# Splitting minus the row maxima into three bfloat16 parts: on VectorE behind the last reduction, or as a queued piece on GpSimd

## The chip, the cores and the metric

The kernel runs on one core of a Trainium2 chip. The metric is the device time of one execution in microseconds. Before the change three runs took 3936.0, 3942.05 and 3945.19 us; the median is 3942.05 us. Engine names below are those of the profile: PE is TensorE, DVE is VectorE, ACT is ScalarE, POOL is GpSimd, SP is the engine whose queue issues most of the DMAs.

## The reference, cut to what matters

One transformer layer over 4 sequences of 2048 tokens, width 256: modulation, layer norm, attention with 16 heads of 16, residual, layer norm, a mixture of 16 experts (4 per token) plus a shared expert, residual. The change touches only the softmax of the attention:

```python
q = _apply_rotary(q, rope)
k = _apply_rotary(k, rope)
scores = jnp.einsum('bhqd,bhkd->bhqk', q, k) * scale
scores = jnp.where(causal_mask, -jnp.inf, scores)
attn = jax.nn.softmax(scores, axis=-1)
out = jnp.einsum('bhqk,bhkd->bhqd', attn, v)
```

The softmax subtracts the maximum of each row of scores before the exponential. The kernel computes that maximum first, in a separate pass over the scores, and then adds its negative to the scores inside the matmul that makes them a second time.

## The kernel before, in words

**Blocks and groups.** The 8192 tokens are 16 blocks of 512 (`n`), four to a sequence. The heads are 4 groups of 4 (`g`). A pair (n, g) is one group of attention work, 64 in all. `units` puts them in order: the first sequence has 16 units of one group each, the other three have units of two groups each.

**A step.** The main loop takes a unit in steps of 128 keys. A step has on PE four small matmuls that add minus the maximum to a PSUM buffer `st` (L1055, from `mt`), four matmuls of the scores (L1062), on ACT two exponentials `e` (L1070), on POOL, for the last four steps of a group only, two triangular masks on `e` (L1074), and, one step late, the matmuls `po` with the values (L1003, in `weigh`). There are 640 steps.

**The maxima.** While a unit runs, the row maxima of the next unit are made beside it, by the generator `row_max`: PE writes scores into a PSUM buffer `ps` (L803, L826), and DVE reduces it to a column of `mparts` (L813, L836). `st` and `ps` share three PSUM buffers of two banks each. `draw` pulls these pieces so that they are spread over the steps of the unit, and what is left is drained at its end. After the last reduction of a group, `row_max` reduces the columns to minus the maximum, `negm` (L849, 128 x 16 numbers), and splits that into three bfloat16 parts in `mb`: round (L857), subtract what was rounded (L859), round the rest (L860), and both once more. Five DVE instructions follow the reduction directly.

**From the parts to the step.** `row_max` then adds a generator `max_rows` to the queue `after_max`. Its first piece does nothing; its second transposes `mb` on PE (`pmx`, L869) and copies the result to `mt` on ACT (L871). The planner pulls one piece of `after_max` at the end of a step, if the credit allows. If a group is about to begin and its `mt` has not been made, the remaining pieces are pulled on the spot.

**The planner.** `Background` holds queues of generators. Before every piece a generator yields what the piece needs: PSUM banks of the small pool `wps` (one buffer), microseconds of DVE, microseconds of POOL. `Budget` adds credit at each step, and `fill` pulls a piece only while the credit it needs is positive. The pieces of `row_max` are pulled by `draw` whatever the credit is, but what they name is taken from it. The other queues are `ahead` (the `prologue` of later blocks: norm, projection, rotation, split into high and low halves, with POOL at L678, L725, L734), `over` and `ends` (dividing and output projection), and `after` (`send`: norm, routing and the scatter of rows by indirect DMAs on POOL, L489). The order of the instructions on PE, ACT, DVE and POOL is what this program emits; each engine works through its own list in that order.

After the attention the expert stage follows, from about 2787 us of the profiled execution on; nothing in it is changed.

Of the kernel before, what the change touches and what calls it, by code (L numbers as in the profile page):

```python
# [14 lines left out]
ALU = mybir.AluOpType  # L15
# [105 lines left out]
def adaln_attention_moe(  # L121
# [17 lines left out]
    nc = tc.nc  # L139
# [457 lines left out]
    with ExitStack() as actx:  # L597
# [38 lines left out]
        mparts, mbs = [], []  # L636
# [154 lines left out]
        def row_max(n, g):  # L791

            qb = n % NQ
            qt, kt = qts[n, g], kts[n, g]
            turn_ = len(turns) % 2
            turns.append((n, g))
            parts = mparts[turn_]
            for q in range(2):

                def scores(ps, t, key, width, to, start=True, stop=True):  # L800
                    for half in range(2):
                        rows = slice(64 * half, 64 * half + 64)
                        nc.tensor.matmul(  # L803
                            ps[:, half, to : to + width],
                            lhsT=qt[rows, q, t * P : (t + 1) * P],
                            rhs=kt[rows, q, key : key + width],
                            start=start,
                            stop=stop,
                            skip_group_check=True,
                        )  # L810

                def best(ps, to, width):
                    nc.vector.tensor_reduce(to, ps[:, :, :width], AX.X, ALU.max)  # L813

                mine = parts[:, 2 * q : 2 * q + 2]
                for kb in range(qb):
                    for t in range(4):
                        yield 0, 1.15, 0
                        ps = psp.tile([P, 2, BT], F32, tag="s", name="ps")
                        scores(ps, t, kb * BT, BT, 0)  # L820
                        best(ps, mine[:, :, t, 2 + kb], BT)
                yield 0, 1.15, 0
                ps = psp.tile([P, 2, BT], F32, tag="s", name="ps")

                for half in range(2):
                    nc.tensor.matmul(  # L826
                        ps[:, half, :],
                        lhsT=idb,
                        rhs=mask.rearrange("p t k -> p (t k)"),
                        start=True,  # L830
                        stop=False,
                        skip_group_check=True,
                    )
                for t in range(4):
                    scores(ps, t, qb * BT + t * P, P, t * P, start=False, stop=(t == 3))
                nc.vector.tensor_reduce(  # L836
                    mine[:, :, :, 0],
                    ps.rearrange("p h (t k) -> p h t k", k=P),
                    AX.X,
                    ALU.max,  # L840
                )
                for t in range(1, 4):
                    yield 0, 0.15 + 0.27 * t, 0
                    ps = psp.tile([P, 2, BT], F32, tag="s", name="ps")
                    scores(ps, t, qb * BT, t * P, 0)
                    best(ps, mine[:, :, t, 1], t * P)
            yield 0, 1.1, 0
            negm = tp.tile([P, 2, 2, 4], F32, tag="negm", name="negm")
            nc.vector.tensor_reduce(  # L849
                negm.rearrange("p q h t -> p (q h) t"),  # L850
                parts[:, :, :, : 2 + qb],
                AX.X,
                ALU.max,
                negate=True,
            )
            mb = mbs[turn_].rearrange("p t (h q e) -> p q h t e", h=2, q=2)
            nc.vector.tensor_copy(mb[:, :, :, :, 0], negm)  # L857
            for part in (1, 2):
                nc.vector.tensor_sub(negm, negm, mb[:, :, :, :, part - 1])  # L859
                nc.vector.tensor_copy(mb[:, :, :, :, part], negm)  # L860
            after_max.add(max_rows(n, g, mbs[turn_]))

        def max_rows(n, g, mb):

            yield 0, 0, 0
            yield 1, 0, 0
            pm = wps.tile([P, 2, BT], BF, tag="w", name="pmx")
            for t in range(4):
                nc.tensor.transpose(pm[:, 0, t * P : (t + 1) * P], mb[:, t, :], idb)  # L869
            mt = tp.tile([P, BT], BF, tag="mt", name="mt", bufs=3)  # L870
            nc.scalar.copy(mt, pm[:, 0, :])  # L871
            mts[n, g] = mt
# [84 lines left out]
        ahead, maxes, after_max, over, ends, after = (Background(budget) for _ in range(6))  # L957
# [4 lines left out]
        load(0)  # L962
        load(1)
        maxes.add(row_max(*units[0][0]))
        maxes.drain()
        after_max.drain()
# [52 lines left out]
        for u, unit in enumerate(units):  # L1019
# [8 lines left out]
            if u + 1 < len(units):  # L1028
                left = max_pieces(units[u + 1])
                for n, g in units[u + 1]:  # L1030
                    maxes.add(row_max(n, g))
# [10 lines left out]
            for s_, (n, g, k_, nkt, off) in enumerate(steps_):  # L1042
# [46 lines left out]
                part = (BT - off) / BT  # L1089
# [412 lines left out]
```

## Time and profile before

| what | value |
|---|---|
| median of three runs | 3942.05 us |
| the profiled execution, its own time | 3947.4 us |
| its span, first to last instruction | 3945.6 us |
| busy: PE, PEld, DVE, ACT, POOL | 84%, 44%, 65%, 39%, 39% of the span |
| attention, 138 to 2787 us of the span | 2649 us |
| groups of attention work | 64 |

PEld is the load of weights on TensorE, which runs beside the matmuls. In the groups of instructions, "x128 | 53.0, 414" reads: 128 instructions, 53.0 us of busy time, 414 ns for one on average. In a timeline, a line gives the start, the time taken, the engine, the line of the kernel, and in brackets how long the engine had been idle and what ended that.

### The profile page before, as it was taken

How to read it: one execution, taken by the hardware profiler on the slowest of the kernel's cores; microseconds unless marked ns; L12 is line 12 of the kernel's file. 1: busy time of each engine (PE TensorE's matmuls, PEld its weight loads, DVE VectorE, ACT ScalarE, POOL GpSimd, SP SyncE). 2: the span in 40 equal slices, each digit the busy share in tenths (PEclk: the TensorE clock that was granted, in tenths of full speed). 3: DMA queues.
4: the chain of work that ended last, by engine and by line, in shares of the span. 5: the costliest groups of instructions: out<-in, count | busy, mean ns of one | idle time of the engine just before them, and what ended most of it. 6: DMA issues, size and time to landing. Idle time of an engine off the chain costs nothing. (4 is left out here: it accounts for less than half of the span.)

```text
span 3945.6 us, 56494 instructions
## 1 busy us (share of the span) xinstructions
PE 3315.9 (84%) x20276; PEld 1727.9 (44%) x20400; DVE 2583.1 (65%) x4644; ACT 1525.7 (39%) x2188; POOL 1531.1 (39%) x2222
## 2 busy tenths in 40 slices
PE   3567888888888989988898888899788889899994
PEld 1223333333334433333433333343377677676662
DVE  1344676767776777767767776677276576667775
ACT  0223344544444544544454454455522222222220
POOL 1223243352434342343425334310146556545555
PEclk7668898988999988988999998899999899899997
DMA  4233233341223322233332222220177567678763
GB/s 168 91 101 115 84 128 112 121 147 54 85 96 125 116 94 91 82 108 117 108 110 100 83 99 81 96 73 28 59 272 243 199 231 250 217 270 303 275 252 139
DMA packets 275115, 544.96 MB, mean 138 GB/s; under 512 B 27534, under 2 KB 143246, under 8 KB 274834
## 3 DMA queue, kind: packets, MB, share of 16 engines
q1 hardware_dynamic: 242578, 454.79, 33.9%
q0 software_dynamic: 27648, 77.63, 5.3%
q10 hardware_dynamic: 4608, 8.91, 0.6%
q8 instruction: 161, 2.64, 0.3%
q14 instruction: 120, 0.98, 0.1%
HBM read 351.42 MB, written 189.81 MB: 137 GB/s over the span
## 5 line engine op out<-in xcount | busy, mean ns | idle before, releaser
L1070 ACT ACTIVATE e<-st 128x1024 f32<-128x1024 f32 (+3 forms) x1280 | 1078.8, 895 | 1039.5 <-PE st L1062 960.3
L813 DVE TENSOR_REDUCE mparts<-ps 128x2 f32<-128x1024 f32 (+3 forms) x1152 | 1180.0, 1044 | 457.1 <-PE ps L803 409.4
L803 PE MATMUL ps<-kt,qt 64*128 64x512 f32 (+3 forms) x3328 | 613.6, 414 | 177.9 <-ACT e L1070 66.7
L1003 PE MATMUL po<-e,vg 128*32 128x512 f32 (+3 forms) x5120 | 670.6, 590 | 29.5 <-POOL e L1074 14.8
L803 PEld LDWEIGHTS ps<-kt,qt 64*128 64x128 f32 x3328 | 303.3, 203 | 769.3 <-ACT e L1070 447.3
L1074 POOL TENSOR_SCALAR_AFFINE_SELECT e<-e 128x256 f32<-128x256 f32 x512 | 204.7, 410 | 952.2 <-ACT e L1070 948.1
L1171 PE MATMUL gu<-xT,wt 128*128 128x256 f32 x1920 | 465.4, 397 | 24.1 <-issue 11.4
L1274 POOL DMA_INDIRECT yd<-yt,to x320 | 315.8, 987 | 390.7 <-ACT hb L1182 208.3
L1062 PE MATMUL st<-qt,kt 64*128 64x512 f32 (+3 forms) x2560 | 462.3, 441 | 0.0
L1171 PEld LDWEIGHTS gu<-xT,wt 128*128 128x128 f32 x1920 | 371.3, 198 | 112.9 <-issue 45.5
L1055 PE MATMUL st<-mt,pick 32*128 32x512 bf16 (+3 forms) x2560 | 302.5, 373 | 79.7 <-DVE mparts L813 49.0
L489 POOL DMA_INDIRECT xs<-row,rowx x256 | 248.4, 970 | 177.7 <-DVE row L480 122.7
L836 DVE TENSOR_REDUCE mparts<-ps 128x8 f32<-128x1024 f32 x128 | 156.7, 1224 | 196.8 <-PE ps L803 181.8
L1062 PEld LDWEIGHTS st<-qt,kt 64*128 64x128 f32 x2560 | 206.2, 199 | 138.5 <-issue 126.7
L725 POOL TENSOR_TENSOR r<-qk,rp 128x512 f32<-128x512 f32 x128 | 164.8, 1306 | 189.3 <-DVE qk L702 185.7
L1270 ACT ACTIVATE yt<-y,of 128x256 f32<-128x256 f32 x160 | 67.1, 470 | 403.5 <-DVE is L1250 213.9
L1055 PEld LDWEIGHTS <-pick 32*128 32x128 bf16 x2560 | 87.4, 92 | 303.2 <-issue 291.1
L1003 PEld LDWEIGHTS po<-e,vg 128*32 128x32 f32 x5120 | 109.2, 112 | 186.9 <-issue 129.1
L678 POOL TENSOR_TENSOR low<-whole,high 128x512 fp32r<-128x512 f32 x64 | 81.4, 1271 | 253.7 <-ACT whole L750 253.7
L1209 PE MATMUL y<-wt,ha 128*128 128x256 f32 x640 | 158.6, 389 | 10.8 <-issue 7.7
L698 PE MATMUL pq<-wqkv,hT 128*128 128x512 f32 x256 | 145.1, 694 | 17.4 <-ACT whole L750 14.9
L1209 PEld LDWEIGHTS y<-wt,ha 128*128 128x128 f32 x640 | 118.6, 195 | 32.7 <-issue 14.7
(209 smaller groups left out, 3603.4 us busy)
## 6 DMA issues: line engine op xcount, KB each, us to landing
wt<-in_w_all SPq DMA_DIRECT2D x160, 640.0 KB
kt<-kd SPq DMA_DIRECT2D x124, 512.0 KB
xt<-xs SPq DMA_DIRECT2D x160, 272.0 KB
qt<-qd SPq DMA_DIRECT2D x64, 512.0 KB
yg<-yd SPq DMA_DIRECT2D x16, 2048.0 KB
vg<-vd SPq DMA_DIRECT2D x124, 168.0 KB
xb<-in_x SPq DMA_DIRECT2D x32, 512.0 KB
qd<-high SPq DMA_DIRECT2D x128, 128.0 KB
```

The source lines that it names most:

```text
L489: s_ = nc.gpsimd.indirect_dma_start(out=ph.xs[:, :], out_offset=bass.IndirectOffsetOnAxis(ap=rowx[:, n, t, j : j + 1], axis=0), in_=row[:, ...
L725: nc.gpsimd.tensor_tensor(r_, parts[:, :, :, s].unsqueeze(2).to_broadcast(full), rp[:, qb * 4 + t, s].unsqueeze(1).to_broadcast(full), ALU ...
L803: nc.tensor.matmul(ps[:, half, to : to + width], lhsT=qt[rows, q, t * P : (t + 1) * P], rhs=kt[rows, q, key : key + width], start=start, s ...
L813: nc.vector.tensor_reduce(to, ps[:, :, :width], AX.X, ALU.max)
L1003: nc.tensor.matmul(po[32 * j : 32 * j + 32, off:], lhsT=va[:, k_, j * (HD + 1) : j * (HD + 1) + 32], rhs=es[j // 2][:, j % 2, off:], start ...
L1055: nc.tensor.matmul(sts[q][:, h_, off:], lhsT=pick[rows, :], rhs=mt[rows, off:], start=True, stop=False,)
L1062: nc.tensor.matmul(sts[q][:, h_, off:], lhsT=kt[rows, q, k_ * P : (k_ + 1) * P], rhs=qt[rows, q, off:], start=False, stop=True,)
L1070: nc.scalar.activation(es[q][:, :, off:], sts[q][:, :, off:], AF.Exp, scale=SCALE)
L1074: nc.gpsimd.affine_select(out=es[q][:, :, off : off + P], in_=es[q][:, :, off : off + P], compare_op=ALU.is_ge, fill=0.0, base=0, pattern= ...
L1171: nc.tensor.matmul(ps[:, c_ * TT : (c_ + 1) * TT], lhsT=wt[:, c_, k * 2 * I + cols : k * 2 * I + cols + P], rhs=xT[:, k, c_ * TT : (c_ + 1 ...
L1209: nc.tensor.matmul(pss[half][:, t, :], lhsT=ha[:, at_ : at_ + P], rhs=wt[:, half, 4 * I : 4 * I + D], start=(t == 0), stop=False, skip_gro ...
L1274: s_ = nc.gpsimd.indirect_dma_start(out=ph.yd[:, :], out_offset=bass.IndirectOffsetOnAxis(ap=to[:, t : t + 1], axis=0), in_=yt[:, t, :], i ...
```

## The change

The five DVE instructions after L849 become five POOL instructions with the same operands, and move from `row_max` into `max_rows`, as a first piece that names 1.2 us of POOL credit. The last piece of `row_max` names 0.2 us of DVE credit where it named 1.1.

```diff
-            yield 0, 1.1, 0
+            yield 0, 0.2, 0
             negm = tp.tile([P, 2, 2, 4], F32, tag="negm", name="negm")
             nc.vector.tensor_reduce(
...
             mb = mbs[turn_].rearrange("p t (h q e) -> p q h t e", h=2, q=2)
-            nc.vector.tensor_copy(mb[:, :, :, :, 0], negm)
+            after_max.add(max_rows(n, g, negm, mb, mbs[turn_]))
+
+        def max_rows(n, g, negm, parts, mb):
+
+            yield 0, 0, 1.2
+            nc.gpsimd.tensor_copy(parts[:, :, :, :, 0], negm)
             for part in (1, 2):
-                nc.vector.tensor_sub(negm, negm, mb[:, :, :, :, part - 1])
-                nc.vector.tensor_copy(mb[:, :, :, :, part], negm)
-            after_max.add(max_rows(n, g, mbs[turn_]))
-
-        def max_rows(n, g, mb):
-
+                nc.gpsimd.tensor_tensor(negm, negm, parts[:, :, :, :, part - 1], ALU.subtract)
+                nc.gpsimd.tensor_copy(parts[:, :, :, :, part], negm)
             yield 0, 0, 0
             yield 1, 0, 0
             pm = wps.tile([P, 2, BT], BF, tag="w", name="pmx")
```

`max_rows` has three pieces where it had two: the parts, an empty one, and the transposes with the copy.

## The prediction

> **What bounds the kernel now.** I read the busy time by stage first.
>
> ```profile
> 138.00:865.00 727.00, 591.13 (x3719) 255.85 (x3747) 452.69 (x666) 298.02 (x391) 231.63 (x292) 0.86 0.31 105
> 865.00:2787.00 1922.00, 1697.41 (x11650) 716.08 (x11745) 1369.10 (x2069) 931.25 (x1190) 682.76 (x1012) 0.91 0.27 93
> ```
>
> The columns are the stretch and its length, busy time of PE, PEld, DVE, ACT and POOL, then granted clock, DMA share and GB/s. The rows are the first sequence and the other three. PE is busy 81% and 88%, DVE 62% and 71%, POOL 32% and 36%: PE carries the attention, and only its idle time (136 and 225 us) can be won or added to. Next, the groups of instructions with shapes kept apart, for what is moved:
>
> ```profile
> L859 DVE TENSOR_TENSOR negm<-negm,mb 128x16 f32<-128x16 f32 x128 | 53.0, 414 | 4.4
> L860 DVE CAST mb<-negm 128x16 bf16<-128x16 f32 x128 | 47.7, 373 | 4.4
> ...
> L857 DVE CAST mb<-negm 128x16 bf16<-128x16 f32 x64 | 28.8, 449 | 2.2
> ```
>
> Together 129.5 us for 320 instructions on 16 numbers a partition. The view of one line (least, median, greatest ns) shows that this is not their own price:
>
> ```profile
> L860 DVE CAST mb<-negm x128: 201/204/1262, 138.6 to 2785.9; 128x16 bf16<-128x16 f32 x128
> ```
>
> The timeline shows where the 1.2 us come from, and what they do to PE:
>
> ```profile
> 1059.90 1.22 DVE L860 CAST mb<-negm 128x16 bf16<-128x16 f32 x1
> 1061.03 3.69 POOL L404 TENSOR_TENSOR row<-row,modb 128x512 f32<-128x512 f32 x3
> ...
> 1061.16 1.17 DVE L859 TENSOR_TENSOR negm<-negm,mb 128x16 f32<-128x16 f32 x1
> 1062.36 1.20 DVE L860 CAST mb<-negm 128x16 bf16<-128x16 f32 x1
> 1063.45 1.21 DVE L813 TENSOR_REDUCE mparts<-ps 128x2 f32<-128x1024 f32 x1
> ...
> 1064.71 0.79 PE L803 MATMUL ps<-kt,qt 64*128 64x512 f32 x2 [5.50 <-DVE mparts L813]
> ```
>
> Each small DVE instruction ends with one of POOL's three of 1.23 us. The next reduction is late by the whole block, and PE stands 5.50 us for the buffer it frees. Read so for all 64 groups, the block from the end of L849 to the end of the last L860 takes 1.14 to 4.47 us, 140.3 us in sum. In the 8 us after the start of L849, PE and PEld are both idle 22.5% of the time, against 13.0% over the attention.
>
> **What goes from DVE.** All five instructions, 140.3 us of DVE time. Only the part counts in which PE waited behind them, found gap by gap in the 48 later groups:
> - PE waits for a reduction queued behind the block: 1.0 + 4.2 (of the 5.5) + 1.65 + twice 2.35 + twice 1.7 = 15.0 us.
> - `pmx` waits for the last L860: 1.9 + 1.4 + 1.9 + 1.1 = 6.3 us; and twice 1.6 for L454, which stands behind the block on DVE: 3.2 us.
> - `st` waits for reductions 4 to 8 us after L849, ten gaps of 0.3 to 0.7: 4.6 us.
>
> That is 29 us. In the first sequence few waits hang on the block; I take 2.7 us there (0.8 before one `pmx`, 1.2 where a routing step on POOL can start earlier, 0.7 from an order that changes).
>
> **What POOL gets.** The trace has no such instruction on POOL. The rows around it:
>
> ```profile
> L725 POOL TENSOR_TENSOR r<-qk,rp 128x512 f32<-128x512 f32 x128 | 164.8, 1306 | 189.3 <-DVE qk L702 185.7 <-DVE den L376 3.6
> ...
> L285 POOL TENSOR_TENSOR rs<-rs,mhalf 128x4 f32<-128x4 f32 x32 | 34.9, 1091 | 231.2 <-DVE rs L284 225.3 <-DVE here L1236 5.8
> ...
> L917 POOL TENSOR_TENSOR obg<-ob,garow 128x256 f32<-128x256 f32 x4 | 2.9, 733 | 0.0
> ```
>
> From 256 to 512 numbers a two-input instruction grows by about 570 ns, so 160 to 180 ns are fixed and 16 numbers cost about 0.21 us (an estimate from these rows). The masks (295 ns at 128, 410 at 256 numbers) give about 0.19 us for a copy in the same way. Three copies, two subtractions, and about 0.08 us at each of four waits on the one before (as between L725 and L734) make **1.4 us**. Below it stands the memset of 16 numbers, 124 ns (0.7 us for five); above it L285, 1.09 us for a power of 4 numbers (5.5 us). I take 1.4: subtract and copy are nearest to L725 and L1074, and a power is another operation. The Trainium skill speaks against the move here: GPSIMD Engine Reference, section Engine selection, says that two-input elementwise work is about twice as slow on GpSimd as on VectorE. Doubling the undisturbed 1.15 us gives 2.3 us, and at the eight places below where the chain is exposed the sum would be some 7 us worse, a gain of 5 instead of 12. I keep the rows, which have the fixed part of a small instruction in them.
>
> 64 x 1.4 = 90 us on an engine with 64% idle time would be nothing, but POOL works in order. What matters is what stands ahead of the parts and behind them. The emitted order shows:
> - In the 48 later groups, 30 have `pmx` one step later, nine two steps later, nine where it was; it keeps at least 3 steps, some 12 us, to its first use. The chain is hidden.
> - In the first 16 groups `pmx` stands, as before, directly ahead of the first step that needs it. In most of these the parts go in ahead of the last step's masks and are ready in time. In the second, third and fourth group they come behind the last masks, and behind more. For the third, from POOL's timeline:
>
> ```profile
> 188.12 0.77 POOL L1074 TENSOR_SCALAR_AFFINE_SELECT e<-e 128x256 f32<-128x256 f32 x2 [4.84 <-ACT e L1070]
> 188.85 1.26 POOL L678 TENSOR_TENSOR low<-whole,high 128x512 fp32r<-128x512 f32 x1
> 190.07 2.57 POOL L725 TENSOR_TENSOR r<-qk,rp 128x512 f32<-128x512 f32 x2
> ```
>
> The parts begin at 192.64 and end at 194.05; transposes, copy and the first `st` take 1.28 us more (as at 157.77 to 159.05), so `st` begins at 195.3 where it began at 190.3: 5.0 us lost. In the same way the second loses 2.9 (behind L285, which ends at 159.20) and the fourth 2.8 (masks until 224.82). Nothing on PE covers this, since `pmx` heads its queue.
> - Two groups have the parts directly ahead of L734, for which PE already waits (2.5 us each): 1.4 each. One group has routing work moved ahead of its L849: 1.5. Four more lose 0.2 to 0.8, together 1.6.
>
> So the first sequence loses 10.7 + 2.8 + 1.5 + 1.6 = 16.6 and wins 2.7: 13.9 us.
>
> **The new waits.** The parts wait on POOL for L849; behind them stand masks, L725 or L734, and scatters L489. The masks also wait for exponentials whose `st` needs a buffer that an earlier reduction frees, so DVE is about at L849 by then. I charge 3 us for the later groups, where PE waits for a mask behind other POOL work (two gaps of 0.4 after L849 at 1105.0, 1.2 + 2.5 at 1678.0). No DMA is in the moved piece. On SP the stores of L678's halves can leave up to 1.4 us later; they are wanted a unit later. The DVE credit (0.9 us a group) lets other DVE pieces in earlier and the POOL credit holds POOL pieces back; the work is the same, and I count it as nothing: up to 8 us either way.
>
> **Sum.** 29 won, 13.9 and 3 lost: 12 us off the profiled 3947.4, so 3935. The profiled execution is 5.4 us above the median of the runs, which gives **3930 us**.
>
> **The rivals.**
> - *No change (0.22, about 3942).* The 29 us are given back: PE gets its buffer earlier and stands for ACT instead, which already holds it 66.7 us at L803 in 122 waits. If half comes back the balance is -2. Against it: the `pmx` gaps have no second releaser.
> - *Slower (0.36, about 3958).* POOL's chain is dear. The place is the starts of the first 16 groups and the eight exposed spots; every us above 1.4 costs about 8 us, so the sign turns at 1.4 + 12/8 = 2.9 us, 0.58 an instruction. At 3.9 us the exposed spots give 20, and boundaries that now have 0.8 to 1.5 us to spare give 8: 16 us slower than before. For it: L285 takes 1.09 us on 4 numbers. Against: memsets and index fills of 4 to 16 numbers take 0.12 to 0.15.
> - *It does not happen.* The planner could leave the piece behind; but the order has 320 more POOL instructions, five for each group. No chance is left for it.
>
> **Chances.** The forecast has 0.42, with its own range 3914 to 3934. About 0.2% (8 us) is what a measurement of this kernel can tell from no change. Faster 0.42, same 0.22, slower 0.36. The range of 8 in 10 reaches from 3912 (all of the 29 us and half of the losses) to 3964 (the dear chain with the reordering against it).
>
> **What would show it.** Right: the five POOL instructions near 0.2 us; PE's wait of 5.5 us near 1060 gone; DVE's busy time in the later 1922 us down by 90 or more; the third group's first `st` about 5 us later after its L849. Wrong: POOL instructions of 0.5 us and more, new PE waits at `pmx` for POOL in the later groups, or DVE's relief answered by longer waits for ACT.

## The result and the profile after

| | before | after |
|---|---|---|
| median of 15 runs | 3937.58 us | 3952.03 us |
| range of the runs | 3925.55 to 3962.94 | 3938.06 to 3969.06 |
| profiled execution | 3947.4 us | 3938.06 us |

The kernel became slower: ratio 1.0035, 95% interval 1.0019 to 1.0052, some 14 us. The forecast was 12 us faster. The single profiled executions stand the other way round (3947.4 and 3938.06), inside a spread of 30 us and more from run to run: the profiled execution of the change is the fastest of its 15 runs. So the traces are used below for where time goes, and repeated runs for how much. Busy time by stage after the change, in the columns used before:

```profile
138.00:865.00 727.00, 574.88 (x3525) 247.92 (x3555) 397.55 (x555) 281.57 (x369) 234.29 (x346) 0.83 0.29 100
865.00:2787.00 1922.00, 1715.50 (x11944) 724.17 (x12033) 1305.71 (x1862) 955.80 (x1226) 765.96 (x1287) 0.93 0.28 95
```

In the same 727 us PE gets through 3525 matmuls where it did 3719, and in the next 1922 us through 11944 where it did 11650. The first sequence has become longer, the rest shorter. Cut by steps and not by time, the first 160 steps take 834.4 us where they took 805.0, and steps 160 to 639 take 1843.0 where they took 1884.5. (Steps are counted by the score matmuls. The idle time below is time in which neither PE nor PEld is busy. One wait in the first part is left out of it everywhere, in which PE's sequencer stands at L803 while the next block's `qt` and `kt` are being loaded: 13.2 us before, 9.9 after, 5 to 14 in all traces. It is shorter where PE was held up more before it.) PE idles 157.6 us in the first part, 132.7 before, and 184.8 in the second, 209.4 before.

The moved instructions, by groups with shapes kept apart:

```profile
L865 POOL CAST mb<-negm 128x16 bf16<-128x16 f32 x128 | 33.6, 262 | 8.3
L864 POOL TENSOR_TENSOR negm<-negm,mb 128x16 f32<-128x16 f32 x128 | 32.3, 252 | 10.5
L862 POOL CAST mb<-negm 128x16 bf16<-128x16 f32 x64 | 18.1, 283 | 122.9 <-DVE negm L849 122.9
```

About 0.25 us each, 84.0 us in sum. From the start of the first to the end of the fifth a group takes 1.51 us (median); 1.4 was estimated. DVE's busy time over the whole execution falls from 2583.1 to 2463.3 us. What PE waits for, from the view of waits over the attention (total us, times, longest), first before the change and then after:

```profile
PE ps L803 <- DVE mparts L813: 31.7, 49, 5.5
PE ptq L739 <- POOL r L734: 19.8, 13, 2.5
...
PE pmx L869 <- DVE mb L860: 11.7, 7, 2.7
...
PE ptq L739 <- DVE negm L859: 6.3, 2, 3.3
```

```profile
PE ptq L739 <- POOL r L734: 35.8, 16, 4.6
PE pt L303 <- DVE xb L290: 19.2, 10, 3.9
PE pmx L870 <- POOL mb L865: 18.9, 9, 4.3
...
PE ps L803 <- DVE mparts L813: 15.9, 39, 1.2
```

The last line is the relief: of seven waits over 0.9 us in the later groups (16.3 us) one of 1.19 is left. The other three are the price. The wait for L734 was 26.1 us: the two that the view before puts down to L859 end within 0.1 us of the end of an L734 (L734 ends at 372.63 and 486.58, PE goes on at 372.69 and 486.64). The wait for the norm's rows was 12.9, and `pmx` waited 11.7 us for DVE's L860. All nine waits of the third line lie in the first sequence. For its third group the timeline shows:

```profile
191.95 2.56 POOL L725 TENSOR_TENSOR r<-qk,rp 128x512 f32<-128x512 f32 x2
194.46 0.25 POOL L862 CAST mb<-negm 128x16 bf16<-128x16 f32 x1
...
195.71 0.25 POOL L865 CAST mb<-negm 128x16 bf16<-128x16 f32 x1
...
196.01 0.61 PE L870 MATMUL pmx<-idb,mb 128*128 128x128 bf16 x4 [4.29 <-POOL mb L865]
...
197.30 0.62 PE L1056 MATMUL st<-mt,pick 32*128 32x512 bf16 x4 [0.67 <-ACT mt L872]
```

The parts come behind the two L725, as the emitted order said, and PE stands 4.29 us. L849 of this group starts at 180.11, against 180.23 before; `st` begins at 197.30 where it began at 190.31:

```profile
190.31 0.40 PE L1055 MATMUL st<-mt,pick 32*128 32x512 bf16 x4
```

### The profile page after: what moved, and what is told of

Same layout as the page of the kernel before. It is cut to its first block, busy times and chain, and to the rows that moved or that the text cites. A ratio compares the mean times of both kernels' runs of the same rounds, so it can differ in the third digit from the quotient of the medians.

```text
span 3936.3 us, 56473 instructions
## 1 busy us (share of the span) xinstructions
PE 3305.8 (84%) x20276; PEld 1723.5 (44%) x20400; DVE 2463.3 (63%) x4324; ACT 1524.4 (39%) x2188; POOL 1611.0 (41%) x2542
## 5 line engine op out<-in xcount | busy, mean ns | idle before, releaser
L813 DVE TENSOR_REDUCE mparts<-ps 128x2 f32<-128x1024 f32 (+3 forms) x1152 | 1180.7, 1044 | 508.6 <-PE ps L803 458.8
L803 PE MATMUL ps<-kt,qt 64*128 64x512 f32 (+3 forms) x3328 | 611.6, 412 | 149.7 <-ACT e L1071 59.1
L1004 PE MATMUL po<-e,vg 128*32 128x512 f32 (+3 forms) x5120 | 671.7, 589 | 28.3 <-POOL e L1075 12.2
L803 PEld LDWEIGHTS ps<-kt,qt 64*128 64x128 f32 x3328 | 301.4, 201 | 738.4 <-ACT e L1071 437.6
L725 POOL TENSOR_TENSOR r<-qk,rp 128x512 f32<-128x512 f32 x128 | 164.9, 1305 | 167.1 <-DVE qk L702 167.1
L678 POOL TENSOR_TENSOR low<-whole,high 128x512 fp32r<-128x512 f32 x64 | 81.3, 1271 | 250.8 <-ACT whole L750 243.5
```

The source lines that it names most:

```text
L725: nc.gpsimd.tensor_tensor(r_, parts[:, :, :, s].unsqueeze(2).to_broadcast(full), rp[:, qb * 4 + t, s].unsqueeze(1).to_broadcast(full), ALU ...
L803: nc.tensor.matmul(ps[:, half, to : to + width], lhsT=qt[rows, q, t * P : (t + 1) * P], rhs=kt[rows, q, key : key + width], start=start, s ...
L1004: nc.tensor.matmul(po[32 * j : 32 * j + 32, off:], lhsT=va[:, k_, j * (HD + 1) : j * (HD + 1) + 32], rhs=es[j // 2][:, j % 2, off:], start ...
```

## The experiments

All use one piece of code: `own` says whether a group's parts are made in the piece of their own; where it is false, DVE makes them as before the change.

```diff
+            own = n >= NQ
-            yield 0, 0.2, 0
+            yield 0, 0.2 if own else 1.1, 0
...
+            if not own:
+                nc.vector.tensor_copy(mb[:, :, :, :, 0], negm)
+                for part in (1, 2):
+                    nc.vector.tensor_sub(negm, negm, mb[:, :, :, :, part - 1])
+                    nc.vector.tensor_copy(mb[:, :, :, :, part], negm)
...
+            if negm is not None:
                 yield 0, 0, 1.2
                 nc.gpsimd.tensor_copy(parts[:, :, :, :, 0], negm)
```

"New amounts" are the 0.2 us of DVE and 1.2 us of POOL that the change names to the planner, "old amounts" 1.1 and nothing. Ratios are to the kernel before on the same chip. The chips differ: the medians of before were 3852.71, 3939.06, 3854.16 and 3934.51 us in the four sessions, so ratios, not times, are compared between sessions.

**First session: which half loses, and to what.** GpSimd for the later sequences only (`own = n >= NQ`):

> The parts are made on GpSimd for the three later sequences only; the first sequence is as before the change. Place theory (the loss is all in the first sequence, where the transposes head PE's queue and the parts stand behind masks and prologue on POOL; the 25 us less idle PE in the later groups are real): 20 to 25 us faster than before the change, ratio about 0.994. Rival (the gain of the later groups in the one profile was a higher granted clock, and PE's earlier buffers are answered by other waits): within 8 us of before, ratio 0.998 to 1.002.

GpSimd for the first sequence only (`own = n < NQ`):

> The other half: GpSimd for the 16 groups of the first sequence only. Place theory: 25 to 30 us slower than before the change, ratio about 1.007, PE idle in the first 160 steps about 158 us where it was 133. Rival (the loss is spread over the kernel): less than 12 us slower.

The planner's amounts alone:

```diff
-            yield 0, 1.1, 0
+            yield 0, 0.2, 0
             negm = tp.tile([P, 2, 2, 4], F32, tag="negm", name="negm")
...
         def max_rows(n, g, mb):
 
+            yield 0, 0, 1.2
             yield 0, 0, 0
```

(The line that is added takes the place of the new piece; nothing is emitted in it.)

> DVE makes the parts where it made them, but the planner is told what it is told after the change: 0.2 us of DVE for the last piece, 1.2 us of POOL for the first piece of the queue behind it. Credit theory (a good part of the first sequence's loss is the other pieces being let in elsewhere): PE idle in the first 160 steps 8 to 12 us more than the 133 of before, and the kernel 5 to 10 us slower. Place theory alone: idle within 3 us of 133 and the time within 4 us of before.

GpSimd with neither a piece of its own nor new amounts:

```diff
-            nc.vector.tensor_copy(mb[:, :, :, :, 0], negm)
+            nc.gpsimd.tensor_copy(mb[:, :, :, :, 0], negm)
             for part in (1, 2):
-                nc.vector.tensor_sub(negm, negm, mb[:, :, :, :, part - 1])
-                nc.vector.tensor_copy(mb[:, :, :, :, part], negm)
+                nc.gpsimd.tensor_tensor(negm, negm, mb[:, :, :, :, part - 1], ALU.subtract)
+                nc.gpsimd.tensor_copy(mb[:, :, :, :, part], negm)
```

> The five instructions go to GpSimd but stay in the last piece of the maxima, directly behind the reduction in the order of emission, and the planner is told what it was told before the change. Place theory: the parts of the second, third and fourth group no longer stand behind the last masks and the prologue's pieces, so most of the first sequence's loss goes: PE idle in the first 160 steps 133 to 142 us, and the kernel 10 to 20 us faster than before the change. If instead GpSimd's waiting for the reduction at that place holds up the masks and L734 behind it, idle is 150 us or more and nothing is won.

| version | ratio, 95% interval | steps 0-160: us, PE idle | steps 160-639: us, PE idle |
|---|---|---|---|
| later sequences | 0.9932 (0.9912 to 0.9953) | 783.6, 126.6 | 1820.9, 183.5 |
| first sequence | 1.0138 (1.0118 to 1.0158) | 832.1, 152.6 | 1855.1, 194.8 |
| amounts only | 1.0029 (1.0012 to 1.0045) | 817.0, 138.7 | 1841.6, 190.8 |
| inline on GpSimd | 1.0053 (1.0033 to 1.0073) | 804.7, 132.6 | 1875.0, 195.8 |

The split is as the place theory has it, and the gain in the later groups is real: 26 us of 3853. The loss is nearly twice what was expected of the second: 1.38% is 53 us. (The two ratios together would make 1.007, and the change has 1.003 to 1.0035; this gap is not explained.) In the second version's trace the first 160 steps are 48.5 us longer than in the first version's, which has the order of before there. Idle time as counted here grows by 26.0 us, and the wait that is left out of it shrinks by 2.4, so busy time for the same matmuls grows by 24.9 us. The amounts alone cost 11 us and account for some 12 of the 26 us of idle time; the order of before itself has 120 to 133 us in six traces. The inline version misses its expectation: little idle time is added in the first sequence, but in the later ones the transposes now wait:

```profile
PE pmx L869 <- POOL mb L860: 27.5, 29, 3.1
```

This is its view of waits over the attention. The wait was 11.7 us in 7 times for DVE. Without a piece of its own, which puts the transposes a step later, there is no gain; but this version lacks the new amounts too (the next session has a gain without them). Only 12 of the 54 us that its later steps take beyond the first version's are idle time.

**Second session: relief or position, and the price of a stall.** The later sequences with old amounts (as the first version, with `yield 0, 1.1, 0` and `yield 0, 0, 0`):

> As the version with GpSimd for the three later sequences only, but the planner is told the old amounts: 1.1 us of DVE for the last piece of the maxima, nothing of POOL for the new piece. If the gain of the later groups is DVE's block and the later transposes, it stays: ratio to before 0.991 to 0.996. If it came from the planner letting other pieces in elsewhere, it goes: ratio 0.998 or more.

A piece of its own in the later sequences, on DVE:

```diff
             if negm is not None:
-                yield 0, 0, 1.2
-                nc.gpsimd.tensor_copy(parts[:, :, :, :, 0], negm)
+                yield 0, 1.1, 0
+                nc.vector.tensor_copy(parts[:, :, :, :, 0], negm)
                 for part in (1, 2):
-                    nc.gpsimd.tensor_tensor(negm, negm, parts[:, :, :, :, part - 1], ALU.subtract)
-                    nc.gpsimd.tensor_copy(parts[:, :, :, :, part], negm)
+                    nc.vector.tensor_sub(negm, negm, parts[:, :, :, :, part - 1])
+                    nc.vector.tensor_copy(parts[:, :, :, :, part], negm)
```

> In the three later sequences the parts are a piece of their own as after the change, but on DVE (0.2 us for the last piece of the maxima, 1.1 us for the new one). Relief theory (the gain of the later groups is that DVE no longer stands in the block): ratio 0.997 to 1.001, PE waits at L803 for L813 about 30 us as before. Position theory (the gain is that the transposes come a step later): ratio 0.992 to 0.995, with the waits at L869 gone.

The first sequence with old amounts:

> GpSimd for the 16 groups of the first sequence only, as in the version that was 1.4% slower, with the old amounts told to the planner. If the place on POOL is one half of that loss and the planner's amounts the other: PE idle in the first 160 steps about 140 us (127 with the order of before, 153 with the new amounts), ratio about 1.006. If the place is all: idle 150 us or more, ratio 1.012 or more.

The first sequence with new amounts and a longer chain:

```diff
                 nc.gpsimd.tensor_copy(parts[:, :, :, :, 0], negm)
+                for _ in range(16):
+                    nc.gpsimd.tensor_copy(parts[:, :, :, :, 0], negm)
```

> GpSimd for the first sequence only, with 16 more copies of the first part in each group, some 4.8 us of chain more; nothing else moves. It prices a stall of PE. Clock theory (a stall of some us lowers PE's granted clock to one half for the 3.4 us stretches that follow, so the matmuls behind it cost extra): the time grows by about 1.8 times the PE idle that is added, and the time at half clock in the first 160 steps grows from 278 us to 320 or more. Plain theory: the time grows by what the idle grows, within 15%, and the half-clock time stays at 265 to 290 us. About 50 us of idle more are expected by both.

| version | ratio, 95% interval | steps 0-160: us, PE idle | steps 160-639: us, PE idle |
|---|---|---|---|
| later, old amounts | 0.9948 (0.9931 to 0.9965) | 804.7, 120.2 | 1863.3, 185.7 |
| later, own piece on DVE | 1.0003 (0.9983 to 1.0023) | 798.9, 128.9 | 1882.5, 194.9 |
| first, old amounts | 1.0079 (1.0049 to 1.0110) | 829.3, 141.5 | 1873.3, 188.1 |
| first, long chain | 1.0300 (1.0272 to 1.0328) | 908.6, 214.2 | 1877.8, 187.9 |

The gain needs no new amounts, and position alone gives nothing: the parts must leave DVE. But the waits that the prediction added up are not the whole of it. The wait at L803 that was expected to stay fell to 15.3 us (31.2 before) over the later sequences even with the piece on DVE, and the waits at `pmx` were gone there. The relief came back as waits for ACT's exponentials (57.4 us, 48.1 before) and at `st` for L813 (57.3, 39.0 before), and the time did not move. The third row is the place without the amounts: about half of the loss, as expected. The long chain refutes the multiplier of 1.8: against the second version of the first session the counted idle time grows by 61.6 us, all idle time by 55.6, and the ratio by 0.0162, some 64 us with an uncertainty of about 13. Long stalls cost about their length. The time at half clock in the first 160 steps did grow, from 267 to 357 us (the expectation's 278 for the former is too high), but 51 of these 90 us lie in idle time, where a slow clock costs nothing.

**Third session: the pieces side by side.**

> GpSimd for all groups but the four of the first block, the planner told the old amounts (1.1 us of DVE, nothing of POOL). If the place on POOL costs most in the first block, where the parts stand behind the last masks and the prologue (10.7 of the 13.9 us of the prediction): ratio to before 0.994 to 0.998, PE idle in the first 160 steps 124 to 132 us. If it costs as much in the other three blocks: ratio 0.999 or more, idle 136 us or more.

> The change with the old amounts told to the planner, in all 64 groups. If the amounts are a good part of the loss of the first sequence: ratio 0.997 to 1.001, PE idle in the first 160 steps about 141 us; the kernel after the change on the same chip 0.3 to 0.6% slower than this. If they are not: the same time as after the change within 0.2%.

> The change as it stands, beside its parts on one chip. Ratio to before 1.002 to 1.006 if the halves add (0.993 and 1.014 on another chip would make 1.007), PE idle 153 to 158 us in the first 160 steps.

> GpSimd for the three later sequences with the new amounts, again, on this chip. Place and credit theories both: ratio 0.993 to 0.996. If the 0.9932 was the other chip's: 0.998 or more.

| version | ratio, 95% interval | steps 0-160: us, PE idle | steps 160-639: us, PE idle |
|---|---|---|---|
| all but the first block, old amounts | 1.0070 (1.0051 to 1.0089) | 827.3, 138.5 | 1848.6, 190.4 |
| all, old amounts | 1.0068 (1.0048 to 1.0088) | 826.2, 137.5 | 1845.7, 192.9 |
| the change | 1.0029 (1.0018 to 1.0040) | 836.9, 152.6 | 1830.6, 176.2 |
| later sequences, new amounts | 0.9906 (0.9887 to 0.9925) | 785.0, 126.6 | 1828.1, 189.3 |

Two expectations miss, and the last version is faster than its expected range. Leaving the first block on DVE wins nothing (first two rows), because with old amounts the parts there no longer stand behind the last masks: the wait of `pmx` for POOL in the first 160 steps is 4.8 us in both, against 16.8 with the change. So it is the amounts named to the planner that hold the piece back until then. (By the program this is the 1.2 us of POOL; the two amounts were not changed one at a time.) And the old amounts are not better but worse over the whole: they save 15 us of idle time in the first part and lose 17 in the second. The loss that remains with old amounts comes with L734. In the last version of the table (later sequences) the timeline shows (line numbers from L849 on are shifted by 1 to 8 in these kernels):

```profile
639.10 0.77 POOL L1082 TENSOR_SCALAR_AFFINE_SELECT e<-e 128x256 f32<-128x256 f32 x2
...
639.83 1.27 POOL L734 TENSOR_TENSOR r<-r,r 128x512 f32<-128x512 f32 x1
...
641.15 0.66 PE L739 MATMUL ptq<-ident,r 128*128 128x128 f32 x4 [2.48 <-POOL r L734]
```

and in the second (all, old amounts), at the same place of the program:

```profile
661.90 0.77 POOL L1082 TENSOR_SCALAR_AFFINE_SELECT e<-e 128x256 f32<-128x256 f32 x2
...
662.62 0.25 POOL L869 CAST mb<-negm 128x16 bf16<-128x16 f32 x1
...
664.03 1.26 POOL L734 TENSOR_TENSOR r<-r,r 128x512 f32<-128x512 f32 x1
...
665.34 0.82 PE L739 MATMUL ptq<-ident,r 128*128 128x128 f32 x4 [3.86 <-POOL r L734]
```

The parts stand between the masks and L734, and PE's wait grows from 2.48 to 3.86 us. Four waits for L734 in the first sequence grow by 1.4 us in this way, and two new ones of 4.5 and 2.6 appear around 757 and 836 us. The last two are not due to the parts' place on POOL alone: with the amounts alone, and the parts on DVE, waits of 3.3 and 2.6 us stand at the same places. What follows the wait, from the busy time by stretches (the eighth number, after the five engines, is the granted clock), first the last version and then the second:

```profile
641.50:648.50 7.00, 6.33 (x31) 2.29 (x29) 1.39 (x7) 2.22 (x5) 1.99 (x3) 0.55 0.35 108
648.50:655.00 6.50, 6.14 (x46) 2.80 (x43) 4.79 (x6) 4.36 (x5) 3.85 (x3) 0.96 0.61 185
```

```profile
665.50:679.20 13.70, 12.18 (x52) 5.41 (x51) 5.74 (x6) 4.64 (x8) 8.44 (x9) 0.51 0.44 142
679.20:686.00 6.80, 6.61 (x48) 2.61 (x48) 6.17 (x9) 3.88 (x4) 0.92 (x1) 0.99 1.04 355
```

Behind the shorter wait PE runs at half clock for some 7 us, behind the longer one for some 14. In the traces the granted clock has two values only, full and half, in stretches of 3.41 us or multiples. The Trainium skill's TensorE: Matmul & The Clock Gate (Part 1: The HAM clock gate) has the same two rates and the same length: half rate after at least one idle window of about 3.4 us, full rate after a busy one. The traces do not bear out that the window must be idle as a whole: the wait of 2.48 us is shorter, and half of 322 drops in five traces follow a stretch of which PE idled less than 47%. Between these two versions the first 160 steps differ by 41.2 us, of which only 10.9 are idle time; half clock in them is 200 and 270 us.

**Fourth session: is the half clock caused by these waits?** Eight extra matmuls fill PE's wait ahead of L739, and leave the rest as it is; their result is overwritten:

```diff
                 pt = wps.tile([P, 4, P], F32, tag="w", name="ptq")
+                for _ in range(8 if n in (1, 2, 3, 5) else 0):
+                    nc.tensor.matmul(
+                        pt.rearrange("p c t -> p (c t)"), lhsT=idb,
+                        rhs=mask.rearrange("p t k -> p (t k)"), start=True, stop=True,
+                    )
```

> The change with the old amounts (all 64 groups on GpSimd, 0.7% slower than before), and eight matmuls of 128x512 bfloat16, some 1.7 us together, written ahead of the rotation's transposes in blocks 1, 2, 3 and 5, into the buffer that the transposes overwrite. They add work to PE where it mostly waits for L734. Clock theory (a wait that leaves PE idle for most of a 3.4 us stretch brings half clock in the stretches behind it, and that is a good part of the first sequence's loss): time at half clock in the first 160 steps falls from about 270 us by 40 or more, and the kernel is faster than the same without the extra matmuls. Plain theory: the half clock stays within 20 us, and the extra matmuls cost 5 to 20 us.

> The change with the old amounts, without the extra matmuls, on the same chip: ratio to before 1.005 to 1.009, half clock in the first 160 steps 255 to 275 us.

> The best version so far (GpSimd for the three later sequences only), with the same eight matmuls in blocks 1, 2, 3 and 5. Clock theory: 5 to 20 us faster than without them, half clock in the first 160 steps under 180 us where it was 192 and 200. Plain theory: 5 to 20 us slower.

> GpSimd for the three later sequences only, without the extra matmuls, on the same chip: ratio to before 0.990 to 0.995.

| version | ratio, 95% interval | steps 0-160: us, PE idle, half clock | steps 160-639: us, PE idle |
|---|---|---|---|
| all, old amounts, filled | 1.0066 (1.0041 to 1.0090) | 830.4, 128.2, 223 | 1868.5, 188.8 |
| all, old amounts | 1.0031 (1.0019 to 1.0044) | 826.4, 143.8, 246 | 1860.8, 183.4 |
| later sequences, filled | 0.9903 (0.9878 to 0.9928) | 809.4, 111.3, 221 | 1853.2, 178.2 |
| later sequences | 0.9936 (0.9918 to 0.9954) | 797.2, 127.4, 222 | 1836.4, 176.0 |

By time alone this settles nothing. Filled, the version with all groups is 0.35% slower and the version with the later sequences 0.33% faster, both with overlapping intervals. The extra matmuls are not free: they keep PE busy for 33.0 and 30.9 us in the two traces, and only some 16 us of that falls into idle time. The all-old version itself is 0.37% nearer to before here than in the third session.

The granted clock, which was measured in every run, says more. A run's time at half clock is twice its span times the part of the clock that it was not granted. Among runs of one version, a run with 10 us more of it takes 3 us longer (slope 0.30, correlation 0.89, over 296 runs in 21 sets of one version in one session). The means over the runs, with standard errors:

| session, version | runs | half clock in a whole run, us |
|---|---|---|
| third: before | 27 | 698, 4 |
| third: the change | 22 | 722, 4 |
| third: all, old amounts | 6 | 722, 6 |
| third: later sequences, new amounts | 6 | 636, 8 |
| fourth: all, old amounts | 22 | 777, 5 |
| fourth: the same, filled | 6 | 764, 6 |
| fourth: later sequences | 12 | 739, 9 |
| fourth: the same, filled | 6 | 679, 17 |

So the fill did lower the half clock of the later-sequences version. Its profiled run does not show it (221 us against 222 in the first 160 steps), but that run is the slowest of the six: 3926.84 us, where the other five took 3884 to 3904. Worked out from these figures (an estimate), the fill should cost 17 - 0.30 x 13 = 13 us in the one version and gain 0.30 x 60 - 15 = 3 in the other; the ratios have 14 slower and 13 faster, within the noise.

The traces show the same price. In the 16 without extra matmuls, PE's busy time in the first 160 steps is 643 to 689 us. It is 579 us plus 0.445 of the part of it that is spent at half clock, to within 5.2 us in each (a fitted line). A matmul of `po` of 128x512 takes 593 ns in the median at full clock and 1061 at half. The order with DVE in the first sequence has 192 to 252 us at half clock there in six profiled executions, the orders with GpSimd pieces there 246 to 275 in seven (without the long chain and the fill); the ranges overlap by one execution each. What half clock costs is shown, then, and that the versions differ in it. Which waits bring it is seen at single places only, and is open.

The fastest version is the one for the later sequences with new amounts: 0.9932, 0.9906 and 0.9936 in three sessions, 25 to 36 us under the kernel before.

## Why the prediction was wrong

**The bound: right. The relief: the number right, in part by luck.** PE was the engine to watch. The five DVE instructions were put at 29 us less 3 in the later groups, and the version that changes only these gains 25 to 36 us. The version with a DVE piece shows that the parts must leave DVE. But the 26 us were meant as idle time. In pairs of traces with and without the move there, steps 160 to 639 have 24.6 us less of it (before and the change), 11.3 (first session) and 2.4 (second session, old amounts). Another 16.9, 22.9 and 7.6 us come from busy time, with 48, 51 and 26 us less at half clock; the prediction had no such term. Part of the relief came back as other waits, as its rival of no change had said.

**The price of the chain: right.** 1.51 us against 1.4 (the prediction's own terms add up to 1.31). The rule of twice VectorE's 1.15 us (2.3) would have been wrong: DVE's subtraction took at least 184 ns, POOL's 224, and a cast 201 and 249. It was also read too widely: that section of the Trainium skill, Engine selection in GPSIMD Engine Reference, says twice for two-input work and roughly line rate for one-input work, and three of the five instructions are copies.

**The first sequence: the mechanism right, its size wrong; this is the step that failed.** The sum let the first sequence lose 16.6 us and win 2.7, together 13.9. The change and the later-sequences version on one chip differ only there, and their ratios by 0.0123, some 47 us; their traces by 51.9 us in the first 160 steps, 22.9 of them idle time and 29.0 busy time. From the views of waits over these steps, the change first, then the later-sequences version:

```profile
PE ptq L739 <- POOL r L734: 26.5, 10, 4.6
...
PE pmx L870 <- POOL mb L865: 16.8, 8, 4.5
```

```profile
PE ptq L739 <- POOL r L734: 12.2, 7, 2.9
...
PE ptq L739 <- DVE negm L861: 6.3, 2, 3.3
...
PE pmx L877 <- DVE mb L862: 2.9, 2, 2.7
```

It divides so:
- Busy time of PE, for the same matmuls: 673.7 where it was 644.6, 29 more. This is the largest term, and the prediction had none for it: it priced a stall at its length. PE's busy time at half clock is 64 us longer, which at 0.445 is 28 us. Over all runs of the two versions the half clock differs by 86 us, which at 0.30 is 26 us of the 47.
- PE idle at `pmx`: 16.8 us for POOL where 2.9 went to DVE, 13.9 more. The prediction had 2.9 + 5.0 + 2.8 + 1.6 = 12.3. Right.
- PE idle for L734: 26.5 where it was 18.5 (12.2, and the two waits put down to L861, which end with L734), 8.0 more. The prediction had 1.4 at two places, 2.8. These two grew as said; it compared the order only around the groups whose L734 had already held PE up, and missed two later places (4.6 and 2.6).
- PE idle at L303 for the norm's rows L290: 14.1 where it was 8.8. This comes with the amounts (14.3 with the amounts alone), which the prediction counted "as nothing: up to 8 us either way". With the amounts alone the idle time of the first part is 138.7, 12.1 more than in the order of before. They also decide where the parts land on POOL: with old amounts the 16.8 us are 4.8.
- A few waits are shorter. One is the wait at L803 that the idle columns leave out, by about 3 us: so something did cover the first stalls, against the prediction's "Nothing on PE covers this".

**The break-even.** The named way to slower was a dear chain. It did not happen; the chain was cheap and the kernel slower all the same, since the first sequence cost more than three times what was put on it.

**Single checks.** Of the three slow DVE instructions near 1060 us the first ends with an L678 of POOL, and only the other two with an L404. The 5.5 us wait is gone, as said, and there is no new wait at `pmx` in the later groups. DVE's busy time in the later 1922 us fell by 63 us, not by 90 or more; more matmuls fall into that stretch now, and over the whole execution it fell by 119.8. The third group's `st` came 7 us later, not 5: POOL was itself 1.8 us late by then. This too is the clock. After the same waits of 2.04 and 1.16 us, these four matmuls ran at full clock before and at half clock after the change:

```profile
185.15 1.98 PE L698 MATMUL pq<-wqkv,hT 128*128 128x512 f32 x4 [1.16 <-ACT whole L750]
```

```profile
185.03 3.78 PE L698 MATMUL pq<-wqkv,hT 128*128 128x512 f32 x4 [1.16 <-ACT whole L750]
```

Counted from the nearest change of the clock, the wait of 2.04 us lies in one stretch of 3.41 us after the change and is shared by two before it. The order of the instructions does not show how a wait will fall into the stretches.

## What to carry to other kernels

Before moving a chain from one engine to another, list what heads whose queue where the chain's result is wanted at once, and what stands directly behind it on the new engine: the chain was hidden in 48 groups and bare in 16, and 16 were enough to lose all. Where the two kinds of place can be told apart, change only the one: the move for three of four sequences is 0.6 to 0.9% faster, the whole is 0.3% slower. Amounts that a planner reads are a change of their own; run them alone. When idle time does not add up to the loss, look at the busy time of the same instructions and at the granted clock of every run, not of one trace.

## What the runs showed of the hardware

- Small GpSimd instructions are cheap: a subtraction of 16 numbers a partition took 224 ns at least and 228 in the median, a cast 252 ns, with some 73 ns between dependent ones; the power of 4 numbers at L285 takes 1.09 us.
- Of PE's busy time at half clock 0.445 was extra: a matmul of `po` of 128x512 took 1061 ns for 593. PE idles in a part of the time at half clock anyway, and a run was longer by 0.30 of that time.
- Chips (each session had its own) differ more than the change does: the kernel before took 3853 us in two sessions and 3935 to 3939 in the others. About 50 us of this is behind step 639 (1063 to 1066 us in the traces of the faster sessions, 1112 to 1120 in the others).
